# First stage of the next image's conv transform: two row combinations on VectorE, GpSimd's later sums behind a gate

## The chip, the cores and the metric

The kernel runs on one core of a Trainium2 chip. The metric is the device time of one execution in microseconds (us); where several executions are timed, the median counts. In what follows PE is TensorE, PEld its weight loads, DVE is VectorE, ACT is ScalarE, POOL is GpSimd, and SP the engine whose queue issues most of the DMAs.

## The reference, cut to what matters

Four images of 256 channels and 48x48 pixels, in float32, pass through two layers; each adds its result to its input.

```python
# layer 0
x = x + proj(attention(qkv(relu(bn(conv3x3(gn(x)))))))      # 8 heads, 2304 tokens per image
# layer 1
g = gn(x)
w = conv3x3(g, W_cat)                                       # 45 maps: 5 dilations x 9 taps
cat = [g] + [sum_k softmax(w_d)[k] * shift(g, tap k of dilation d) for d in (1, 6, 12, 24, 36)]
x = x + batchnorm(conv1x1(concat(cat), W_scale))            # statistics over all four images
```

`gn` is a group norm over groups of 8 channels. `bn` uses given statistics, the last batch norm those of its own input.

## The kernel before

**Stages.** The images go through a software pipeline. For each image b there is a conv with the qkv products (`conv_qkv`), then attention (`attention`), then the filters of layer 1 (`dynamic_filters`). Two of these overlap: while the filters of image b-1 are computed, the conv and qkv of image b are the stream `other`, from which `run(ns)` and `drive` pull matmuls to fill TensorE. So there are three changes from one attention to the next mixed stage, after the attention of images 0, 1 and 2. I call them transitions. After the attention of image 3 only the filters are left (`alone`).

**The conv of images 1 to 3** (`Blocks`, `conv_blocks`) is done in a transformed domain in both directions. Rows first: `self.d` holds six views of the normalized image (every fourth row, offset 0 to 5, each 2 x 12 x 50 elements per partition), and `stage0`, `scaled` and `rest` combine them into six row results `v[0]` to `v[5]`, with `v[6]` as scratch. Then columns: `along(i)` forms from `v[i]` four arrays (j = 1, 2, 0, 3), which are the moving operands of the matmuls for row result i (L1178). The order of i is `ORDER = (1, 2, 3, 4, 0, 5)`; each i takes two tiles (the two halves of the output channels), each tile four steps j, each step two matmuls into one of two PSUM buffers (tag "c"). A step's result is taken out by ACT for the first j (`one`, L1193) and by DVE for the others (L1203, L1204, L1214, L1216). The stream hands back control twice a step, after each matmul, and reports 486 ns each time; a tile is 8 such pieces.

**Where stage0 runs.** `following[0]` is called in `attention` after the last matmuls on the numerators and ahead of `close(last)`, which normalizes the last part of the attention (two DVE transposes around a reciprocal, L1420 to L1430). It builds `Blocks` and calls `stage0` (L1022). In it ACT multiplies two views by 4 (L1025, L1026), and POOL does everything else through `sum` (L1018, two instructions each, one per half of the channels) and `along` (L1096, four instructions): v[3], v[0], v[5], v[1], then the column sums of v[1], then v[2]. The row results live in the memory of the old q and k, so all this waits until the last scores of the attention are done.

**What follows on TensorE.** The last chunk of the projection (L1465), the statistics of the group norm of layer 1 (`norm.finish`: L675 for the mean, L686 and L687 for the variance, with ACT and DVE work between), the normalization of the image in place (two parts of 24 rows; DVE takes one half of the channels, L648, ACT the other, L2116), and then the weights conv (L1547), which needs the whole normalized image. Between these steps `run` pulls conv matmuls: 1000 ns after the local statistics (three matmuls), 1000 ns after the mean (three), 1900 ns after the first part of the normalization (four), 2900 ns after the second (six). These are 16 matmuls, two tiles, all with i = 1. The column sums of the second row result, `along(ORDER[1])`, are issued in the first of those tiles (in `conv_blocks`, at the first matmul), so they stand on POOL's queue right behind stage0. After that `drive` takes over: it runs several streams, each with its own due times from a hand-kept clock (`Clock`), and the order of instructions on every engine is fixed by it when the kernel is built. `rest` is one of these streams.

Of the kernel before, what the change touches and what calls it, by code (L numbers as in the profile page):

```python
# [8 lines left out]
F32 = mybir.dt.float32  # L9
F32R = mybir.dt.float32r  # L10
AF = mybir.ActivationFunctionType
ALU = mybir.AluOpType
# [3 lines left out]
B, C, HH, WW = 4, 256, 48, 48  # L16
N = HH * WW
P = 128
# [40 lines left out]
def conv_preact_kernel(  # L59
# [12 lines left out]
    nc = tc.nc  # L72

    const = ctx.enter_context(tc.tile_pool(name="const", bufs=1))
    small = ctx.enter_context(tc.tile_pool(name="small", bufs=2))
# [477 lines left out]
    with tc.tile_pool(name="w", bufs=1) as wpool, tc.tile_pool(  # L553
        name="act", bufs=1
# [432 lines left out]
        class Blocks:  # L987
# [34 lines left out]
            def stage0(self):  # L1022

                v, d = self.v, self.d
                nc.scalar.mul(v[0], d[2], 4.0)  # L1025
                nc.scalar.mul(v[5], d[1], 4.0)  # L1026
                self.sum(v[3], d[4], d[2], ALU.subtract)
                self.sum(v[0], d[4], v[0], ALU.subtract)
                self.sum(v[5], d[3], v[5], ALU.subtract)
                self.sum(v[1], v[0], v[5], ALU.add)  # L1030
                self.along(1)
                self.sum(v[2], v[0], v[5], ALU.subtract)

            def scaled(self):

# [74 lines left out]
        def conv_blocks(b, psum_tile, blocks, pool, hid):  # L1110

            axpy = blocks.axpy
            tt = nc.vector.tensor_tensor
            rows = hid.rearrange("p h (t r w) -> p h t r w", r=4, w=WW)
            spare = list(blocks.spare)

            results, last = [], [0.0]

            def busy_dve():
                return clock.t["DVE"] > max(clock.t["ACT"], clock.t["PE"]) + 500  # L1120

            def relu(o, r, y, end):
                results.append((o, r, y, end))

            def relus(limit):
                while results and results[0][3] + 150 <= limit:
                    o, r, y, end = results.pop(0)
                    nc.scalar.activation(  # L1128
                        rows[:, o, :, r, :], rows_of(y), AF.Relu,
                        bias=bn_t[:, o : o + 1], scale=bn_s12[:, o : o + 1],  # L1130
                    )
                    clock("ACT", 660, end)

            def before(i, o):

                s12, d12, s34, d34 = (blocks.held[:, j, o] for j in range(4))
                if i == 0:
                    t = spare.pop(0)
                    axpy(t, s34, -4.0, s12)
                    relu(o, 2, t, clock.both(800))  # L1140
                    either(s12, s12, s34, ALU.subtract)
                elif i == 5:
                    t = spare.pop(0)
                    axpy(t, d34, -2.0, d12)
                    relu(o, 1, t, clock.both(800))
                    axpy(d12, d34, -8.0, d12)
                    clock.both(800)

            def target(i, o):

                if i in (1, 3):
                    return blocks.first[o]
                if i in (2, 4):
                    return blocks.held[:, 1 if i == 2 else 3, o]
                return spare.pop(0)

            def after(i, o, y):

                s12, d12, s34, d34 = (blocks.held[:, j, o] for j in range(4))
                if i in (2, 4):  # L1160
                    s, d = (s12, d12) if i == 2 else (s34, d34)
                    either(s, y, blocks.first[o], ALU.add)
                    either(d, blocks.first[o], y, ALU.subtract)
                elif i in (0, 5):
                    relu(o, i and 3, y, either(y, y, s12 if i == 0 else d12, ALU.add))

            blocks.scaled()
            need[0] = lambda: 150 + max(slot("c", 2), blocks.end[STEPS[0]])
            for t, (i, o) in enumerate(TILES):
                u = us.pop(t)  # L1170
                y = target(i, o).rearrange("p (n s) -> p n s", s=2)
                for n, j in enumerate((1, 2, 0, 3)):
                    m = psum_tile(f"pc_{b}_{i}_{o}_{j}")[:, :XN]
                    clock("PE", 0, slot("c", 2), blocks.end[i, j])
                    z = blocks.of[i].rearrange("p (j h n) -> p j h n", j=4, h=NH)[:, j]
                    relus(max(clock.t["ACT"], clock.t["PE"]))
                    for h in range(NH):
                        nc.tensor.matmul(  # L1178
                            m, u[:, h, j], z[:, h], start=(h == 0), stop=(h == NH - 1)
                        )  # L1180
                        clock("PE", MM * XN / CH)
                        if h == 0:
                            need[0] = lambda: 0.0
                            if n == 0:
                                if t + 2 < len(TILES):
                                    us[t + 2] = taken(t + 2)
                                if t == 0:
                                    blocks.along(ORDER[1])
                                before(i, o)
                            yield MM * XN / CH  # L1190
                    if n == 0:
                        one = pool.tile([P, XN], F32, tag="one", name=f"one_{b}_{i}_{o}")
                        nc.scalar.copy(one, m)  # L1193
                        end = clock("ACT", 400, clock.t["PE"])
                    elif n == 1:
                        two = pool.tile([P, 2, XN], F32, tag="two", name=f"two_{b}_{i}_{o}")
                        if busy_dve():
                            nc.scalar.copy(two[:, 1], m)
                            end = clock("ACT", 400, clock.t["PE"])
                            either(two[:, 0], one, two[:, 1], ALU.add, end)  # L1200
                            either(two[:, 1], one, two[:, 1], ALU.subtract, end)
                        else:
                            tt(two[:, 0], m, one, ALU.add)  # L1203
                            tt(two[:, 1], one, m, ALU.subtract)  # L1204
                            end = clock("DVE", 900, clock.t["PE"], end)
                    else:
                        to = y[:, :, n - 2]
                        if busy_dve():
                            nc.scalar.mul(to, m, 1.0 if j == 0 else -1.0)
                            end = clock("ACT", 450, clock.t["PE"])  # L1210
                            either(to, to, two[:, n - 2], ALU.add, end)
                        else:
                            if j == 0:
                                tt(to, m, two[:, 0], ALU.add)  # L1214
                            else:
                                tt(to, two[:, 1], m, ALU.subtract)  # L1216
                            end = clock("DVE", 480, clock.t["PE"])
                        if n == 3:
                            after(i, o, y.rearrange("p n s -> p (n s)"))
                    free["c"].append(end)  # L1220
                    then = STEPS[4 * t + n + 1] if 4 * t + n + 1 < len(STEPS) else None
                    need[0] = lambda: 150 + max(
                        slot("c", 2), blocks.end.get(then, NEVER) if then else last[0],
                    )
                    if n == 3 and o == NH - 1:
                        blocks.passed.add(i)
                    if then is None:
                        relus(NEVER)
                        last[0] = clock.t["ACT"]
                    yield MM * XN / CH  # L1230
# [253 lines left out]
        def dynamic_filters(b, ao, chunk, norm, other, pools):  # L1484
# [621 lines left out]
                project(b, chunk, ao, pp, norm)  # L2106
                chunk += 1
            table(AF.Sqrt)
            for _ in norm.finish(misc):
                run(1000)  # L2110
            norm.shift_of()
            for part in range(2):
                for h in range(NH):
                    t = inside(gn, h, HH // 2 * part, HH // 2)
                    if h:
                        nc.scalar.activation(  # L2116
                            t, t, AF.Identity, bias=norm.shift[:, h : h + 1],
                            scale=norm.rstd[:, h : h + 1],
                        )
                    else:  # L2120
                        normalize(t, t, norm.mean, norm.rstd, h)
                run((1900, 2900)[part])
                if alone and part == 0:
                    flag_of(misc("pf")[:1, : B * NH])
            clock.level()
# [542 lines left out]
```

## Time and profile before

| | |
|---|---|
| median of 3 runs | 2685.55 us (2680.86 to 2685.71) |
| the profiled execution's own time | 2688.87 us |
| its span, first to last instruction | 2687.1 us |
| PE busy | 2595.5 us (97%) |
| DVE busy | 2077.2 us (77%) |
| ACT busy | 1809.1 us (67%) |
| POOL busy | 809.7 us (30%) |
| mean granted TensorE clock | 0.989 |

The profile is of one execution. A row of the timeline has the start in us from the span's start, the length, the engine, the line of the kernel, the operation, what is written and read with sizes, and how many instructions are merged in it; in brackets stands how long the engine had been idle before it, and what ended that. A matmul in float32 appears as two records. A row of the waits has the waiting engine and line, the releaser, and the total, the count and the longest. A row of windows has the busy time of each engine in that stretch (number of instructions in brackets), then the granted TensorE clock as a share of full speed, the DMA share and GB/s.

### The profile page before, as it was taken

The page shows a single profiled execution, that of the slowest core. Times are in us where ns is not written, and L with a number is a line of the kernel's source. Part 1 is how long each engine was busy: PE and PEld are TensorE (multiplying, and loading weights), DVE is VectorE, ACT ScalarE, POOL GpSimd, SP SyncE. Part 2 cuts the span into 40 slices and gives each one's busy share as a digit, 9 for nine tenths or more (in the row PEclk, how much of TensorE's full clock was granted, in tenths as well). Part 3 has the DMA queues.
Part 4 walks back from the last instruction along what each step waited for, and adds up shares of the span by engine and source line. Part 5 has one row for each costly group of instructions (what it writes and reads, how often), then busy time and mean ns, then how long its engine had stood idle before and what let it go on. Part 6 is the DMA issues. An engine that isn't in the chain of part 4 may idle for free. (4 is left out here: it accounts for less than half of the span.)

```text
span 2687.1 us, 42567 instructions
## 1 busy us (share of the span) xinstructions
PE 2595.5 (97%) x16952; PEld 1097.6 (41%) x16952; DVE 2077.2 (77%) x2033; ACT 1809.1 (67%) x2287; POOL 809.7 (30%) x893
## 2 busy tenths in 40 slices
PE   7999999999999999999999999999989999999996
PEld 5632222555562222355555222245546222235554
DVE  7768898758739998957774988894776889895676
ACT  4479898734449999854445998984444889885344
POOL 4201100476520001067750001007765010100453
PEclk9999999999999999999999999999999999999998
DMA  4815445323253445423324354442324544432456
GB/s 173 227 38 107 102 101 117 89 63 103 69 108 73 101 105 110 101 73 86 94 66 90 90 112 102 102 104 78 82 74 119 135 100 101 102 88 76 122 165 221
DMA packets 138094, 279.96 MB, mean 104 GB/s; under 512 B 58152, under 2 KB 98512, under 8 KB 136864
## 3 DMA queue, kind: packets, MB, share of 16 engines
q0 software_dynamic: 27408, 144.00, 23.3%
q1 hardware_dynamic: 110480, 133.17, 18.4%
q8 instruction: 135, 2.21, 0.3%
q14 instruction: 71, 0.58, 0.1%
HBM read 112.12 MB, written 36.04 MB: 55 GB/s over the span
## 5 line engine op out<-in xcount | busy, mean ns | idle before, releaser
L1392 DVE TENSOR_TENSOR acc<-acc,p 128x2048 f32<-128x2048 f32 (+1 forms) x568 | 1039.3, 1830 | 96.2 <-ACT p L1353 44.2
L1353 ACT ACTIVATE p<-se 128x1536 f32<-128x1536 f32 x648 | 937.6, 1447 | 0.0
L1342 PE MATMUL se<-q,k 32*128 32x512 f32 (+1 forms) x4320 | 737.1, 593 | 0.0
L1342 PE MATMUL so<-q,k 32*128 32x512 f32 (+1 forms) x1440 | 728.3, 593 | 3.2 <-DVE bound L1297 2.0
L1377 PE MATMUL num<-p,vT 128*32 128x512 f32 (+1 forms) x5760 | 699.4, 561 | 1.7 <-ACT ao L1402 1.7
L1352 ACT ACTIVATE p<-so 128x512 f32<-128x512 f32 x648 | 388.9, 600 | 158.8 <-PE se L1342 63.1
L1845 POOL TENSOR_TENSOR near<-near,prod 128x384 f32<-128x384 f32 x352 | 353.2, 1036 | 254.8 <-DVE prod L1839 248.8
L1342 PEld LDWEIGHTS so<-q,k 32*128 32x128 f32 x1440 | 216.5, 183 | 517.8 <-ACT p L1352 477.0
L1396 POOL DMA_DIRECT2D ring<-p x128 | 109.2, 853 | 800.9 <-ACT p L1353 589.4
L1377 PEld LDWEIGHTS num<-p,vT 128*32 128x32 f32 x5760 | 128.9, 108 | 475.1 <-issue 448.5
L1839 DVE TENSOR_TENSOR prod<-wb,pad 128x768 f32<-128x768 f32 x192 | 182.0, 954 | 84.9 <-ACT wb L1826 54.1
L1342 PEld LDWEIGHTS se<-q,k 32*128 32x128 f32 x4320 | 227.2, 183 | 5.1 <-ACT p L1353 4.3
L1826 ACT COPY wb<-ws 128x384 f32<-128x384 f32 x216 | 108.5, 505 | 164.9 <-DVE prod L1839 124.2
L1394 POOL DMA_DIRECT2D ring<-p x36 | 20.2, 560 | 569.5 <-ACT p L1353 284.8
L2003 PE MATMUL py<-far,wsc 128*128 128x384 f32 x512 | 169.9, 487 | 0.0
L1547 PE MATMUL pg<-pad,wcat 128*45 128x384 f32 x864 | 147.8, 493 | 8.5 <-ACT lg L1605 8.5
L1258 PE MATMUL pq<-hid,wqkv 128*128 128x384 f32 x384 | 132.7, 500 | 14.2 <-ACT hid L1128 12.0
L1515 ACT COPY far<-far 128x512 f32<-128x512 f32 x86 | 90.3, 1108 | 81.4 <-PE far L1773 77.9
L2003 PEld LDWEIGHTS py<-far,wsc 128*128 128x128 f32 x512 | 96.2, 190 | 66.0 <-issue 1.8
L1258 PEld LDWEIGHTS pq<-hid,wqkv 128*128 128x128 f32 x384 | 73.1, 194 | 68.4 <-ACT hid L1128 14.3
L1392 DVE TENSOR_TENSOR acc<-p,p 128x2048 f32<-128x2048 f32 x36 | 82.3, 2285 | 21.5 <-ACT p L1353 14.6
L1747 DVE COPY_PREDICATED amat<-along_y,bmat 128x768 f32<-128x768 uint32 x72 | 94.7, 1315 | 2.4
(336 smaller groups left out, 2874.0 us busy)
## 6 DMA issues: line engine op xcount, KB each, us to landing
ring<-p POOLq DMA_DIRECT2D x164, 768.0 KB, 5.7
ws<-w_d SPq DMA_DIRECT2D x216, 192.0 KB
ring<-u_d SPq DMA_DIRECT2D x36, 512.0 KB
pad<-in_x SPq DMA_DIRECT2D x14, 1152.0 KB
xst<-in_x POOLq DMA_DIRECT2D x36, 192.0 KB, 3.5
x_d<-pad SPq DMA_DIRECT2D x36, 192.0 KB
u_d<-pad SPq DMA_DIRECT2D x12, 512.0 KB
y_d<-y SPq DMA_DIRECT2D x13, 384.0 KB
```

The lines of the kernel that those rows point to most:

```text
L1258: nc.tensor.matmul(pq[:, :CH], wqkv[:, i, s, g * P : (g + 1) * P], hid[:, i, cols], start=(i == 0), stop=(i == NH - 1),)
L1342: nc.tensor.matmul(dst[:, at : at + n], k_[r, g, m * P : (m + 1) * P], q[r, g, q0 : q0 + n], start=True, stop=True,)
L1352: nc.scalar.activation(p[:, 0, :], s1, AF.Exp, scale=QS)
L1353: nc.scalar.activation(p[:, 1:, :], s3, AF.Exp, scale=QS)
L1377: nc.tensor.matmul(st["num"][r, at : at + n], vT[:, m, g * P + j * D : g * P + (j + 1) * D], p[:, j, at : at + n], start=(m == 0 and not s ...
L1392: nc.vector.tensor_tensor(st["acc"][:, js], other[:, js], p[:, js], ALU.add)
L1396: nc.gpsimd.dma_start(out=extra, in_=p[:, 1:], accum_op=ALU.add)
L1547: nc.tensor.matmul(pg[64 * s : 64 * s + NG, :CH], wcat[:, ii, k, :], shifted(ii, cc, k // 3 - 1, k % 3 - 1), start=(i == 0 and k == 0), st ...
L1826: nc.scalar.copy(pw[:, :CH], fetched[c, k][0])
L1839: nc.vector.tensor_tensor(prod.rearrange("p h (r w) -> p h r w", w=WW), wb, src, ALU.mult)
L1845: nc.gpsimd.tensor_tensor(cat[:, h], cat[:, h], prod[:, h], ALU.add)
L2003: nc.tensor.matmul(py[c][:, o, :CH], wsc[:, n * NH + i, o * P : (o + 1) * P], rhs, start=(n == 0 and i == 0), stop=(n == order[-1] and i = ...
```

## The change

Four edits. (1) In `stage0`, v[0] = d[4] - 4 d[2] and v[5] = d[3] - 4 d[1] are each computed by two DVE instructions (scalar_tensor_tensor) instead of an ACT multiplication and two POOL subtractions; v[3] goes to the end of the stage. (2) `along(ORDER[1])` is issued in the last step of the second tile instead of the first step of the first. (3) Where another conv is running beside the filters, the first `run` of the norm takes 2500 ns (six matmuls) instead of 1000 (three), and the last takes 1400 ns (three) instead of 2900 (six); the total of 16 stays. (4) After the second part of the normalization is issued, one POOL instruction on a single element per partition reads one element of the first and one of the last row that DVE normalizes, so that POOL waits there until both parts are done.

```diff
             def stage0(self):
 
                 v, d = self.v, self.d
-                nc.scalar.mul(v[0], d[2], 4.0)
-                nc.scalar.mul(v[5], d[1], 4.0)
-                self.sum(v[3], d[4], d[2], ALU.subtract)
-                self.sum(v[0], d[4], v[0], ALU.subtract)
-                self.sum(v[5], d[3], v[5], ALU.subtract)
+                self.axpy(v[0], d[2], -4.0, d[4])
+                self.axpy(v[5], d[1], -4.0, d[3])
                 self.sum(v[1], v[0], v[5], ALU.add)
                 self.along(1)
                 self.sum(v[2], v[0], v[5], ALU.subtract)
+                self.sum(v[3], d[4], d[2], ALU.subtract)
...
                         if h == 0:
                             need[0] = lambda: 0.0
+                            if t == 1 and n == 3:
+                                blocks.along(ORDER[1])
                             if n == 0:
                                 if t + 2 < len(TILES):
                                     us[t + 2] = taken(t + 2)
-                                if t == 0:
-                                    blocks.along(ORDER[1])
                                 before(i, o)
...
             table(AF.Sqrt)
-            for _ in norm.finish(misc):
-                run(1000)
+            for i, _ in enumerate(norm.finish(misc)):
+                run(1000 if i or alone else 2500)
             norm.shift_of()
...
-                run((1900, 2900)[part])
+                if part:
+                    gate = small.tile([P, 1], F32, tag="gate", name=f"gate_{b}")
+                    nc.gpsimd.tensor_tensor(
+                        gate, gn[:, 0, 1, 1:2], gn[:, 0, HH, 1:2], ALU.add
+                    )
+                run((1900, 2900 if alone else 1400)[part])
```

`axpy`, called by stage0 now, existed already: for each half of the channels it issues `nc.vector.scalar_tensor_tensor(out, in0=x, scalar=a, in1=y, op0=mult, op1=add)`.

## The prediction on record

> **What bounds the kernel now.** The page first. Its row of busy times says that TensorE has little to give:
>
> ```profile
> PE 2595.5 (97%) x16952; PEld 1097.6 (41%) x16952; DVE 2077.2 (77%) x2033; ACT 1809.1 (67%) x2287; POOL 809.7 (30%) x893
> ```
>
> PE idles for 92 us in all, so an edit pays only where PE waits. The waits of PE sorted by cause name the place: `PE pc L1178 <- POOL cv_v L1096`, 7.1 us in 3 times, one per transition. The PE timeline of the first transition, from the projection (L1465) to the weights conv (L1547), shows it:
>
> ```profile
> 519.35 2.85 PE L1465 MATMUL pp<-ao,wp 128*128 128x384 f32 x8
> 524.58 1.86 PE L1178 MATMUL pc<-cv_v,ring 128*128 128x288 f32 x6 [2.38 <-POOL cv_v L1096]
> 526.27 0.28 PE L675 MATMUL pm_n<-mvn,gmat 128*128 128x2 f32 x2
> 526.41 1.70 PE L1178 MATMUL pc<-cv_v,ring 128*128 128x288 f32 x6
> 527.95 0.28 PE L686 MATMUL pv_n<-mvn,gmat 128*128 128x2 f32 x2
> ...
> 531.77 3.45 PE L1178 MATMUL pc<-cv_v,ring 128*128 128x288 f32 x12 [1.27 <-DVE cv_k L1216]
> 535.15 2.16 PE L1547 MATMUL pg<-pad,wcat 128*45 128x384 f32 x12
> ```
>
> The bracket on the second row is the gap: the projection ends at 522.20, the first conv matmul starts at 524.58. POOL's timeline says why:
>
> ```profile
> 511.14 4.04 POOL L1018 TENSOR_TENSOR cv_k<-pad 128x600 f32<-128x600 f32 x2 [9.09 <-issue]
> 515.14 5.32 POOL L1018 TENSOR_TENSOR cv_q<-pad,cv_q 128x600 f32<-128x600 f32 x4
> 520.42 2.86 POOL L1018 TENSOR_TENSOR cv_k<-cv_q 128x600 f32<-128x600 f32 x2
> 523.36 4.53 POOL L1096 TENSOR_TENSOR cv_v<-cv_k 128x576 f32<-128x576 f32 x4
> ```
>
> From top to bottom: v[3], then v[0] and v[5], then v[1], then its column sums; without pause, so the first column sum is ready only at 523.36 + 1.17. From DVE's timeline, the slack and the normalization:
>
> ```profile
> 510.08 2.29 DVE L1392 TENSOR_TENSOR acc<-acc,p 128x2048 f32<-128x2048 f32 x1
> 516.13 0.72 DVE L1420 STREAM_TRANSPOSE rt<-den 128x512 f32<-128x512 f32 x1 [3.76 <-PE den L1408]
> ...
> 529.14 2.21 DVE L648 TENSOR_SCALAR pad<-pad,gmean_n,grstd_n 128x1152 f32<-128x1152 f32 x1
> ```
>
> DVE is free from 512.37 to 516.13. Its L648 takes 2.21 here, and by its list of durations 0.86 to 2.21 for one shape: POOL is running beside it. Last, the busy times by stretch for the second transition; the column to see is the third from the right, the granted clock:
>
> ```profile
> 1171.50:1173.70 2.20, 0.00 (x0) 0.00 (x0) 2.13 (x4) 0.00 (x0) 2.12 (x3) 1.00 0.28 61
> 1173.70:1179.00 5.30, 5.22 (x17) 3.83 (x17) 1.29 (x5) 1.07 (x5) 5.30 (x6) 0.68 0.50 148
> ```
>
> In half-microsecond stretches the clock is 0.50 from about 1175.0 to 1178.3. The third transition has the same after its gap (0.69), the first has not (1.00).
>
> **What the Trainium skill says.** "TensorE: Matmul & The Clock Gate", Part 1: TensorE falls to half clock after an idle window of about 3.4 us, the window is free-running, and full clock returns after a busy one. The trace agrees on the length (3.3 us at 0.50) and on the element of chance (two of three like gaps), but gaps of 2.36 us were enough. "SBUF — State Buffer", Who interferes with whom: a DVE instruction with two SBUF inputs, or a tensor_scalar in a two-port mode, and a GpSimd instruction that reads SBUF exclude each other for the whole instruction. The trace agrees: L1076, the DVE form that the change adds, takes 0.75 us (128x576) and up to 1.55, and L648 spreads as said.
>
> **The change, part by part.** I count from the end of the projection to the start of L1547. Before: T1 522.20 to 535.15 = 12.95; T2 1171.42 to 1185.59 = 14.17; T3 1824.22 to 1837.73 = 13.51; sum 40.63 us.
>
> *v[0] and v[5] on DVE.* Four instructions of 128x600. Nearest rows: L1076 0.75 for 576 elements, L877 0.78 for 600 with two SBUF inputs. I take 0.775, so 3.1 us, in the 3.76 us ahead of the transpose; queued behind them is `close(last)`, for which PE waits. POOL has nothing to do until the third one ends (512.37 + 2.33 = 514.70), so only the fourth can collide with it; if that takes 1.55 the transpose starts 0.1 to 0.2 late. I take 0.15 per transition. Ends: 0 (as now) and, if all four take 1.55, 6.2 - 3.76 = 2.4. ACT loses two multiplications of 1.21, worth nothing: it idles 6.7 us right after.
>
> *POOL's start.* v[1] at 514.8, two of 1.46 plus at most 0.8 of collision: done by 518.5; the first column sum 1.17 later, 519.7. PE needs it at 522.20, so 2.5 us of cover, and the next sums come every 1.17 while PE uses one per 1.13. The gap goes.
>
> *Matmuls reordered.* From 524.58 to 526.27 three conv matmuls take 1.69: 0.563 each. Now, from the projection's end: six, 3.38; mean matmuls 0.14 (526.27 to 526.41); some 0.1 for the buffer that DVE frees with L1204; three, 1.69; the variance matmuls start at 5.31 and take 0.36; three more reach 7.36. The seventh after the variance needs the buffer that ACT's L1193 frees, and that stands behind ACT's first half of the normalization. Before, L686 started at 527.95 and this L1193 ended at 531.29, 3.34 later; so now at 8.65 to 8.71. PE waits 1.35, then four matmuls, 2.25: L1547 could start at 10.96. The wait for L1216 (1.27 in T1) is thus not saved but replaced. The local statistics that the mean matmuls need end at 524.95 = 2.75, hidden by the six matmuls.
>
> *Gate and held sums.* L648's second part follows L1204 at about 9.55; with POOL held it takes 0.86 to 1.36: 10.4 to 10.9, just inside. Without the gate it could take 2.2, and L1547 would be 0.8 late; that is what the gate is worth. Queued behind the gate on POOL: `along(ORDER[1])` (4.6 us) and `rest` (first six sums 8.9). Gate at about 533.1 in T1, so they end at 546.6 instead of 545.05. The first to need the sums is the third tile at 545.53, now some 2 us sooner: they are ready at 537.7, 6 us of cover. After `rest`'s third result POOL is next released at 551.87 (by DVE), now about 550: 3.4 us of cover. The gate itself is one element. DMAs: the weights of the second tile land by 517.5 (525 needed); the DMAs that tiles issue on SP keep their places. The build clock gets the same POOL additions ahead of `drive`, so I expect the same order after it.
>
> *Sum.* 10.96 + 0.15, rounded to 11.1, three times: 33.3 against 40.63: 7.3 us, of which T1 1.85, T2 3.07, T3 2.41. Of it half clock: the six matmuls around the mean took 4.76 in T2 and 4.63 in T3 against 3.23 in T1, so 1.53 + 1.40 = 2.93. The profiled execution, 2688.87 (1.8 around its span), would become 2681.6. It lies 3.3 above the median of the runs, which may well hold fewer half-clock windows. I count the 4.4 that don't depend on the clock and about 2.1 of the 2.9: 2685.55 - 6.5 = **2679.0**.
>
> **Does it last?** In the conv stage behind each transition the waits of PE are small (largest there: L1258 for ACT 2.2 to 6.1, L1547 2.3), and all follow PE's own work; so a shift lasts until attention, where ACT and PE go in step.
>
> **The rivals.** About 0.2% (5.4 us) is what a measurement can tell from no change here.
>
> *Larger:* the 1.35 wait for L1193 doesn't arise, because ACT or the buffers come earlier than I read. 3 x 1.35 = 4.05 more: **2675.0**. For it: T3 before waits only 0.36. Against: ACT's order is fixed, 0.48 + 1.35 us stand ahead.
>
> *Given back as half clock elsewhere:* 0.50 also shows near 645, 735, 1230, 1385, 1865 and 1950, a window costing about 3.3 x 0.5 = 1.7. Shifts move the work against the windows; one more per mixed stage gives back 5.1: **2684.1**. Against: it may as well go the other way.
>
> *Slower: the DVE work is not covered.* If the four instructions take 1.55, `close` and the projection move 2.4 us, the gap only moves ahead of the projection, and all three transitions pay half clock: 3 x (10.96 + 2.44) = 40.2, with 3 x 1.5 for the clock (as above) 44.7 against 40.63: **2689.6**. It decides from 0.94 us each, where 3.76 is used up, and loses from about 1.4. For it: L1076 beside POOL. Against: POOL has nothing to read before the third ends.
>
> *The change doesn't do what it says:* if POOL began late because the DVE results wait for the numerators' end (516.9), the first sum would be there at about 524, saving nearly nothing; but POOL began at 511.14 on the same memory, so I give this no chance of its own.
>
> **How the numbers follow.** Likeliest (2676 to 2682) 0.58; larger 0.15; given back 0.21; slower 0.06. Faster by over 0.2% (under 2680.2): 0.45 of the likeliest, all of the larger, 0.02 of the given back: 0.62. Slower by over 0.2% (above 2690.9): 0.04. The rest 0.34. The range runs from 2674.5 to 2685.0; outside lie half of the larger, the slower case and 0.06 of the given back.
>
> **What would show it.** PE's row behind L1465 without a bracket, and its start within 0.1 of the projection's end; four DVE rows between L1392 and L1420, with L1420's idle time near 0.6 and its start at most 0.2 late against L1392; clock 1.00 at all three transitions; L1547 11.1 after the projection's end; a wait of about 1.35 for ACT L1193; L648 at 0.86 to 1.36; POOL's `along` behind L648. Wrong would be: L1420 over a microsecond late, PE waiting for POOL at the third tile (L1096 into hid), or transitions shorter as said with the sum gone.

## The result and the profile after

| | before | after |
|---|---|---|
| median | 2685.06 us (14 runs, 2680.02 to 2688.80) | 2677.47 us (14 runs, 2673.73 to 2681.37) |
| profiled execution, span | 2688.87, 2687.1 | 2675.02, 2673.2 |
| granted TensorE clock, mean | 0.989 | 0.992 |
| projection's end to L1547 (after: L1545), T1 / T2 / T3 | 12.95 / 14.17 / 13.51 | 10.61 / 10.61 / 10.61 |

The medians lie 7.6 us apart. The ratio after to before is 0.9974, interval 0.9966 to 0.9981, which is 7.0 us (5.1 to 9.1): faster by a little over the 0.2% that can be told. Ratios leave out runs more than 1.5% above a kernel's fastest; in e1 and e2 below these are taken for the runs that show the effect most, so there I go by the median and the spread of all runs. Behind `stage0` the lines of the kernel after stand two lower: L1465 is L1463, L1178 is L1176, L1547 is L1545.

PE's timeline of the first transition after the change; in the brackets, how long PE had been idle and what ended that:

```profile
519.17 2.85 PE L1463 MATMUL pp<-ao,wp 128*128 128x384 f32 x8
521.86 3.07 PE L1176 MATMUL pc<-cv_v,ring 128*128 128x288 f32 x12
524.84 0.38 PE L675 MATMUL pm_n<-mvn,gmat 128*128 128x2 f32 x2
525.60 1.69 PE L1176 MATMUL pc<-cv_v,ring 128*128 128x288 f32 x6 [0.38 <-DVE two L1202]
527.12 0.28 PE L686 MATMUL pv_n<-mvn,gmat 128*128 128x2 f32 x2
...
527.49 1.70 PE L1176 MATMUL pc<-cv_v,ring 128*128 128x288 f32 x6
530.49 2.21 PE L1176 MATMUL pc<-cv_v,ring 128*128 128x288 f32 x8 [1.30 <-ACT one L1191]
532.63 2.16 PE L1545 MATMUL pg<-pad,wcat 128*45 128x384 f32 x12
```

The conv matmul behind the projection has no bracket any more: the 2.38 us for POOL are gone. In the place of the 1.27 us for L1216 stand 1.30 us for ACT, and 0.38 us for DVE's L1202 are new. POOL and DVE at the same time:

```profile
514.43 3.29 POOL L1018 TENSOR_TENSOR cv_k<-cv_q 128x600 f32<-128x600 f32 x2 [12.58 <-DVE cv_q L1074]
517.80 4.52 POOL L1094 TENSOR_TENSOR cv_v<-cv_k 128x576 f32<-128x576 f32 x4
522.28 2.92 POOL L1018 TENSOR_TENSOR cv_k<-cv_q 128x600 f32<-128x600 f32 x2
525.15 2.89 POOL L1018 TENSOR_TENSOR cv_k<-pad 128x600 f32<-128x600 f32 x2
532.16 0.19 POOL L2122 TENSOR_TENSOR gate<-pad 128x1 f32<-128x1 f32 x1 [4.12 <-DVE pad L648]
532.31 4.80 POOL L1094 TENSOR_TENSOR hid<-cv_k 128x576 f32<-128x576 f32 x4
```

```profile
512.11 2.86 DVE L1074 SCALAR_TENSOR_TENSOR cv_q<-pad 128x600 f32<-128x600 f32 x4
515.95 0.72 DVE L1418 STREAM_TRANSPOSE rt<-den 128x512 f32<-128x512 f32 x1 [0.98 <-PE den L1406]
...
528.30 0.88 DVE L648 TENSOR_SCALAR pad<-pad,gmean_n,grstd_n 128x1152 f32<-128x1152 f32 x1
530.47 0.46 DVE L1201 TENSOR_TENSOR two<-pc,one 128x288 f32<-128x288 f32 x1 [1.29 <-ACT one L1191]
```

POOL starts v[1] 2.3 us behind the start of the first DVE row (before: 520.42, now 514.43), v[1]'s sums start at 517.80 instead of 523.36, and POOL is still from 528.04 to 532.16, held by the gate while DVE normalizes in 0.88. The row of busy times by stretch for the second transition has the clock third from the right, now 1.00:

```profile
1169.00:1174.00 5.00, 4.62 (x23) 3.41 (x21) 3.82 (x10) 1.07 (x5) 5.00 (x4) 1.00 0.66 179
```

**Where the time went.** The three transitions lost 8.80 us (40.63 to 31.83). The two profiled executions differ by 13.9; in stretches of 5 us, the one before had about three more with a clock below 0.99 elsewhere, at about 1.7 each, which makes up the rest. The medians differ by 7.6. Outside the transitions, and `stage0` just ahead of them, every engine has the same instructions in the same order in the two profiles, but for one gate more after the attention of image 3.

### The profile page after: what moved, and what is told of

The parts are those of the page before. It is cut to its first block, busy times and chain, and to the rows that moved or that the text cites. A ratio compares the mean times of both kernels' runs of the same rounds, so it can differ in the third digit from the quotient of the medians.

```text
span 2673.2 us, 42578 instructions
## 1 busy us (share of the span) xinstructions
PE 2586.6 (97%) x16952; PEld 1092.1 (41%) x16952; DVE 2080.8 (78%) x2045; ACT 1802.6 (67%) x2281; POOL 789.6 (30%) x885
## 3 DMA queue, kind: packets, MB, share of 16 engines
q8 instruction: 135, 2.21, 0.3%
## 5 line engine op out<-in xcount | busy, mean ns | idle before, releaser
L1545 PE MATMUL pg<-pad,wcat 128*45 128x384 f32 x864 | 146.7, 490 | 8.8 <-ACT lg L1603 8.8
```

The source lines that it names most:

```text
L1545: nc.tensor.matmul(pg[64 * s : 64 * s + NG, :CH], wcat[:, ii, k, :], shifted(ii, cc, k // 3 - 1, k % 3 - 1), start=(i == 0 and k == 0), st ...
```

## The experiments

Two theories. **A**, the one on record: the gain is the early start of v[1] plus the new order of the matmuls, and the gate is worth 0.8 us at most. **B**: the gate does more than that, or the rows on DVE cost more than I saw. All runs are timed beside the kernel before on the same chip; its median there lay between 2683.4 and 2685.9. There were four chips: one for e1 to e4, one for e7 to e10, one for e6, e11 and e12, one for e13. Comparisons between these groups are comparisons across chips.

### e1: the rows alone

```diff
-                nc.scalar.mul(v[0], d[2], 4.0)
-                nc.scalar.mul(v[5], d[1], 4.0)
-                self.sum(v[3], d[4], d[2], ALU.subtract)
-                self.sum(v[0], d[4], v[0], ALU.subtract)
-                self.sum(v[5], d[3], v[5], ALU.subtract)
+                self.axpy(v[0], d[2], -4.0, d[4])
+                self.axpy(v[5], d[1], -4.0, d[3])
...
+                self.sum(v[3], d[4], d[2], ALU.subtract)
```

Against the kernel before; edits 2 to 4 are left out.

> Only the first edit: v[0] and v[5] by DVE, v[3] last; the matmuls are taken 3, 3, 4, 6 as before, no gate. Theory (each edit has its own wait): the gap of 2.4 us behind the projection goes and the half clock with it, but three matmuls end 1.7 us after the projection and the local statistics only at 2.75, so PE waits about 1.0 for DVE L672 ahead of the mean matmuls; and L648 runs beside POOL (up to 2.2 us), so the wait for L1214 of about 1.3 stays. From the projection's end to the weights conv 11.9 us per transition, against 10.61 with all edits: about 4 us slower than the changed kernel, 3 to 6 faster than the one before. Rival (the DVE rows alone are the gain): 10.6 per transition, as fast as the changed kernel.

Measured: median 2695.65 us (22 runs, 2675.56 to 2722.78), slower than before. But the runs lie in groups: ten from 2675.6 to 2684.1, six from 2695.3 to 2698.9, five from 2707.3 to 2712.7, one at 2722.8. The profiled execution was of the first group (2681.58): transitions of 11.54 to 11.57 and this wait ahead of the mean matmuls, which edit 3 covers:

```profile
525.00 0.38 PE L675 MATMUL pm_n<-mvn,gmat 128*128 128x2 f32 x2 [1.36 <-DVE mvn L672]
```

So of the 8.8 us, edit 1 saves 6.0 (40.63 to 34.66), when nothing happens. In 12 runs of 22 something costs 12 to 16 us, once or more; no profile holds it here, e2 shows what it is likely to be.

### e2: rows and order, no gate

```diff
...
-                if part:
-                    gate = small.tile([P, 1], F32, tag="gate", name=f"gate_{b}")
-                    nc.gpsimd.tensor_tensor(
-                        gate, gn[:, 0, 1, 1:2], gn[:, 0, HH, 1:2], ALU.add
-                    )
```

Against the kernel after, of which edits 1 and 3 are left: edit 2 is undone too (the lines left out above are those shown at e9). By the code, POOL's order without the gate is the same whether edit 2 is made or not; this was not run.

> Edits one and three: DVE rows and the matmuls taken 6, 3, 4, 3, no gate, so that POOL forms the second column sums while DVE normalizes. Theory: the waits ahead of the mean go; L648 takes 1.4 to 2.2 instead of 0.88, its second part ends about 0.5 to 1.3 later, and since the weights conv stands right behind it, a transition takes 11.1 to 11.7 instead of 10.61: 1.5 to 3 us slower than the changed kernel. Rival (the gate does nothing, POOL would not hit DVE there): 10.6, no difference.

Measured: median 2703.05 us (16 runs, 2676.15 to 2722.59). The profiled execution (2687.24) caught it once, in the first transition. PE, DVE and POOL there:

```profile
529.09 1.24 PE L1176 MATMUL pc<-cv_v,ring 128*128 128x288 f32 x4 [1.30 <-ACT one L1191]
540.95 2.29 PE L1176 MATMUL pc<-cv_v,ring 128*128 128x288 f32 x4 [10.62 <-DVE two L1202]
543.17 3.29 PE L1545 MATMUL pg<-pad,wcat 128*45 128x384 f32 x12
```

```profile
526.89 13.28 DVE L648 TENSOR_SCALAR pad<-pad,gmean_n,grstd_n 128x1152 f32<-128x1152 f32 x1
```

```profile
526.57 4.56 POOL L1094 TENSOR_TENSOR hid<-cv_k 128x576 f32<-128x576 f32 x4
531.04 2.89 POOL L1018 TENSOR_TENSOR cv_v<-cv_v,cv_q 128x600 f32<-128x600 f32 x2
533.85 2.89 POOL L1018 TENSOR_TENSOR cv_q<-cv_k,cv_v 128x600 f32<-128x600 f32 x2
536.66 2.89 POOL L1018 TENSOR_TENSOR cv_k<-cv_k,cv_v 128x600 f32<-128x600 f32 x2
```

One instruction of 0.88 us took 13.28. It could not run until POOL had gone through ten instructions one behind another and its queue was empty, at 539.55. PE's bracket of 10.62 names DVE's L1202, which was queued behind it. The transition is 22.6 instead of 10.6, and the clock from 541 to 546, behind so long a gap, is 0.55. In the other two transitions of the same execution L648 took 1.48 and all was well (10.61), with the same instructions ahead of it; so it isn't for a result of POOL's that it waits. This is a **lock-out**, and A is wrong on what the gate is worth. The experiments from e9 to e13 ask what makes it and what ends it.

### e9: the sums of v[2] ahead of the gate

```diff
-                            if t == 1 and n == 3:
-                                blocks.along(ORDER[1])
...
+                                if t == 0:
+                                    blocks.along(ORDER[1])
```

Against the kernel after; edit 2 is undone.

> The changed kernel without the later call of the column sums of v[2]: they stand ahead of the gate on GpSimd instead of behind it. If VectorE is locked out until GpSimd's queue pauses, the lock-out now ends at the gate: L648 at most about 5 us (the four sums take 4.5) instead of 13, and TensorE waits at most 2 to 3 us for it. The median is then 2677 to 2685, with a spread of no more than 10 us and no step of 13. Rival: the gate has no part in ending the lock-out, or the place of the sums has no part in it: either steps of 13 us again (2690 or more), or the changed kernel's own time, 2677, with L648 at 0.9.

Measured: 2691.02 us (10 runs, 2684.16 to 2692.70), ratio 1.0024 (1.0014 to 1.0034). The lock-out is bounded, as expected, but it seems to come nearly always (the profiled execution, 2684.16, is the fastest of the ten and holds two) and it costs more than I wrote: those two transitions take 13.1, and behind the one below the clock is down to 0.72 (1182 to 1186). DVE, POOL and PE in the second transition:

```profile
1173.77 4.86 DVE L648 TENSOR_SCALAR pad<-pad,gmean_n,grstd_n 128x1152 f32<-128x1152 f32 x1
```

```profile
1173.46 4.55 POOL L1094 TENSOR_TENSOR hid<-cv_k 128x576 f32<-128x576 f32 x4
1180.22 0.19 POOL L2122 TENSOR_TENSOR gate<-pad 128x1 f32<-128x1 f32 x1 [2.22 <-DVE pad L648]
```

```profile
1179.40 1.24 PE L1176 MATMUL pc<-cv_v,ring 128*128 128x288 f32 x4 [2.21 <-DVE two L1202]
```

L648 ends 0.6 us after the fourth sum, just where POOL stops at the gate. So POOL's pause ends it; and edit 2, which by the code changes nothing alone, keeps the four sums of v[2] from L648. It doesn't keep stage0 from it: in e6 below, where v[3] ends later, the first part of L648 took 1.9 in spite of the gate.

### e8: v[3] ahead of v[2], no gate

```diff
-                self.sum(v[2], v[0], v[5], ALU.subtract)
                 self.sum(v[3], d[4], d[2], ALU.subtract)
+                self.sum(v[2], v[0], v[5], ALU.subtract)
```

Against e2.

> The second experiment (VectorE's rows and the new order, no gate) with two GpSimd steps exchanged: v[3] ahead of v[2]. Then the column sums of v[2] follow directly on the instruction whose result they read and must wait for its end, as in the kernel before. Theory: VectorE's L648 is locked out for 13 us only when GpSimd has a run of instructions none of which waits for the one directly ahead of it; here it gets in at the latest between v[2] and its sums, within 2.9 us. Then no steps of 13 us: L648 at most 3 us, all runs within about 8 us of each other, median 2677 to 2682. Rival: the lock-out is a matter of chance whenever GpSimd is busy, or of the new moment at which L648 starts, and v[3]'s place has no part in it: L648 of 10 us or more in some transitions, runs again spread over 2676 to 2722 with steps of 13 us, median 2690 to 2705.

Measured: 2678.06 us (22 runs, 2674.91 to 2681.93), ratio 0.9979 (0.9973 to 0.9986). No steps; L648 at most 1.60. On the chip of e9, exchanging two POOL steps does what the gate does. POOL's rows of the first transition:

```profile
525.31 2.87 POOL L1018 TENSOR_TENSOR cv_k<-cv_q 128x600 f32<-128x600 f32 x2
528.26 5.57 POOL L1094 TENSOR_TENSOR hid<-cv_k 128x576 f32<-128x576 f32 x4
```

v[2] ends at 528.18 and its sums start at 528.26: they wait 0.08 for the result directly ahead. In e2 the sums follow on v[3] without such a gap (v[3]'s row ends at 526.64, theirs starts at 526.57). One thing doesn't fit my wording, though: L648 came at 528.45, after that wait, in the middle of four sums that wait for nothing, and got in at the next boundary all the same. So it may be the wait, or the moment at which L648 comes: 0.2 us after the start of the first sum here, 0.3 in e2. e11 keeps the moment of e2, e12 takes a third one.

### e11: one pause, no gate

```diff
                         self.end[i, j] = clock("POOL", 1400)
+                        if i == ORDER[1] and j == js[0]:
+                            stop = small.tile([P, 1], F32, tag="stop", name=f"stop_{self.b}")
+                            nc.gpsimd.tensor_tensor(
+                                stop, to[:, 0, 0, 0:1], to[:, 0, 0, 1:2], ALU.add
+                            )
```

Against e2.

> The second experiment (rows and order, no gate, GpSimd's order as in the change, so with lock-outs) with one GpSimd instruction of a single element added behind the first of the four column sums of v[2]; it reads that sum, so GpSimd must wait for the end of the instruction directly ahead, once. L648 arrives 0.3 us after the start of that sum. Theory: the lock-out lasts as long as GpSimd's instructions follow without such a wait, and any one wait ends it. Then L648 gets in at the wait, about 0.8 us after it arrives, and takes at most about 1.8 us; no run above 2685, median 2677 to 2680, though nothing holds GpSimd back for VectorE. Rival: the wait is too short to matter, and only an empty or a held queue ends the lock-out: L648 of 10 to 13 us in some transitions, runs spread from 2676 to 2722, median 2690 to 2705.

Measured: 2678.48 us (14 runs, 2675.92 to 2680.61), ratio 0.9982 (0.9974 to 0.9990); L648 at most 1.53. The whole pause, on POOL:

```profile
528.04 1.16 POOL L1094 TENSOR_TENSOR hid<-cv_k 128x576 f32<-128x576 f32 x1
529.28 0.59 POOL L1098 TENSOR_TENSOR stop<-hid 128x1 f32<-128x1 f32 x1
529.83 3.91 POOL L1094 TENSOR_TENSOR hid<-cv_k 128x576 f32<-128x576 f32 x3
```

From 529.20 to 529.28: 0.08 us without a POOL instruction, and DVE, waiting since 528.32, got in. Nothing was held back until DVE was done. L648 came 0.3 us after the start of the first sum in all three transitions, as in e2. On this chip no kernel ran in which lock-outs were to be expected, so e11 alone doesn't exclude that it has none; but e8, free, and e9, not free, ran on one chip.

### e12: another moment

> The matmuls handed out as in e7 and GpSimd's order as in e8, without the gate. L648 then starts about 0.4 us later than in e8, some 0.5 us after the first column sum of v[2] instead of 0.2. If what kept e8 free of lock-outs is the wait ahead of these sums as such, this one is free as well: median 2674 to 2676, ratio 0.9963, no run above 2682. If it is only the moment at which L648 arrives within GpSimd's instruction (0.2 us after its start in e8, 0.3 us in the experiments with lock-outs), they come back here: runs in steps of 12 to 14 us, median 2680 to 2700. L648 at 1.2 to 1.6 us where it gets in.

The edit is e7's (below) and e8's together, without the gate. Measured: 2674.88 us (6 runs, 2670.61 to 2678.18), ratio 0.9969 (0.9957 to 0.9981), L648 at most 1.14. It came 0.65 to 0.67 us after the start of the first sum, against 0.2 in e8 and 0.3 in e2 and e9. So being free isn't bound to the moment of e8. Together with e11, which is free at the moment of e2, this speaks for the wait and against the moment; e12 alone wouldn't, since it avoids 0.3 as well.

### e10: the kernel before, v[3] last

```diff
-                self.sum(v[3], d[4], d[2], ALU.subtract)
...
                 self.sum(v[2], v[0], v[5], ALU.subtract)
+                self.sum(v[3], d[4], d[2], ALU.subtract)
```

> The kernel before with one line moved: GpSimd computes v[3] behind v[2] instead of first. Nothing goes to VectorE, no order of TensorE changes, no gate. Theory (lock-out behind a run of GpSimd instructions that don't wait for the one directly ahead): L648 of some 10 to 13 us in some transitions, runs in steps of 13 us from 2685 up to 2725, median 2690 to 2710, though less work has moved than in any other experiment. Rival (the lock-out came with VectorE's new rows or with the earlier start of GpSimd's work): no L648 over 3 us, median 2684 to 2687, ratio within 0.1% of 1.

Measured: 2681.20 us (14 runs, 2679.41 to 2700.09). Twelve runs lie from 2679.4 to 2683.5, two at 2698.0 and 2700.1; 39 runs of the unedited kernel beside it reach no more than 2690.8. A median 3 us lower, since v[1] is ready sooner (in T1 PE's gap behind the projection is 1.31 instead of 2.38), and two runs some 18 us slower. That is far rarer than the expected text has it (median 2690 to 2710), and the profile holds no lock-out, so that these two were lock-outs is inferred from the size of the step. If they were, lock-outs are possible without the wait ahead of the run, but v[3]'s place alone doesn't make them frequent: 12 runs of 22 in e1 and 15 runs of 16 in e2 had a step. What does is not shown.

### e13: L648 in another form

```diff
-                        normalize(t, t, norm.mean, norm.rstd, h)
+                        nc.vector.scalar_tensor_tensor(
+                            out=t, in0=t, scalar=norm.mean[:, h : h + 1],
+                            in1=norm.rstd[:, h : h + 1].unsqueeze(2).to_broadcast(
+                                [P, HH // 2, WW]
+                            ),
+                            op0=ALU.subtract, op1=ALU.mult,
+                        )
```

Against e2.

> The second experiment (rows and order, no gate, no pause, the order in which lock-outs came) with L648 issued in another form: a scalar_tensor_tensor that subtracts the mean and multiplies by the reciprocal deviation as a broadcast operand, instead of a tensor_scalar. GpSimd's queue is unchanged. Theory: only some forms of VectorE's instruction have to wait for GpSimd (in the traces L648, a tensor_scalar, and the copy L1515 are stretched beside GpSimd, the tensor_tensors L1201 and L1202 are not, 0.44 to 0.46 us in all of them). Then the new form takes the same time whatever GpSimd does, an estimated 1.2 to 1.5 us from the 0.78 us of 600 elements at L1074, and nothing is ever locked out: median 2677 to 2680, no run over 2685. Rival: any instruction of VectorE of this size can be locked out: durations of 10 us or more, runs spread to 2722, median 2690 to 2705.

My theory fell. Median 2706.12 us (6 runs, 2700.05 to 2723.43), and the profiled execution (2719.74) has a lock-out in each transition:

```profile
528.26 13.88 DVE L2119 SCALAR_TENSOR_TENSOR pad<-pad,gmean_n,grstd_n 128x1152 f32<-128x1152 f32 x1
...
1188.45 13.89 DVE L2119 SCALAR_TENSOR_TENSOR pad<-pad,gmean_n,grstd_n 128x1152 f32<-128x1152 f32 x1
...
1851.56 13.87 DVE L2119 SCALAR_TENSOR_TENSOR pad<-pad,gmean_n,grstd_n 128x1152 f32<-128x1152 f32 x1
```

The mistake was to count L1201 and L1202 as witnesses: they read one operand from PSUM. The new form reads two from SBUF, and of that the Trainium skill ("SBUF — State Buffer", Who interferes with whom) says that it contends with a GpSimd instruction that reads SBUF, just as the two-port tensor_scalar does. The run agrees. With POOL idle the new form takes 1.41 and L648 0.88, so a form that was slower by itself was shut out just as long.

### e3: the change without the rows, and e4: the gap filled

e3 keeps edits 2 to 4 and leaves `stage0` as it was. e4 is the kernel before with four matmuls on constants in the gap:

```diff
             table(AF.Sqrt)
+            if not alone:
+                busy(misc(f"fill_{b}"), 4)
```

> The changed kernel with stage0 as before (ACT and POOL form v[0] and v[5]); order, later column sums and gate stay. Theory: PE waits 2.4 us again behind the projection, with half clock in some transitions; a transition takes 2.4 + 10.6 = 13.0 us, as before (12.95) or a little more with the clock: within 2 us of the kernel before. Rival (order and gate carry the gain): 3 us or more faster than before.

> The kernel before with four idle matmuls (results unused, about 1.9 us) behind the projection in the three transitions, so that PE has no gap of 2.4 us there but starts the conv no sooner. Theory (the gap causes the half clock): clock 1.00 in all transitions, about 12.9 to 13.0 us per transition, and of the 7.6 us of the change only the half clock's share comes: 2 to 3 us faster than before. Rival (half clock comes by chance anywhere, the gap is not its cause): half clock still in some transitions, time as before.

Measured: e3 2689.26 us (22 runs), ratio 1.0016 (1.0010 to 1.0022), with transitions of 12.83, 14.35 and 14.22, and half clock in the last two (0.69 and 0.66 over the stretch): order and gate are worth nothing until v[1] comes sooner. By the ratio e3 is 4.3 us slower than before, where within 2 was expected; its profiled transitions are only 0.8 longer in sum, and where the rest lies was not followed. e4 2681.32 us (22 runs), ratio 0.9988 (0.9982 to 0.9995), though the conv matmuls still start late (12.92, 12.92, 13.29). The rows by stretch, from the first of them on, have the clock at 1.00 in T2 and T3, where before it was 0.68 and 0.69:

```profile
1174.70:1180.00 5.30, 5.30 (x25) 4.09 (x25) 2.64 (x8) 2.17 (x9) 5.30 (x5) 1.00 0.48 138
1825.60:1831.00 5.40, 5.40 (x26) 4.13 (x26) 2.74 (x8) 2.24 (x9) 5.40 (x5) 1.00 0.49 141
```

So keeping PE busy over the gap, with work of no use, is worth 0.0012 of 2685, 3.2 us (1.3 to 4.8; the medians lie 4.6 apart). I had counted 2.1 for it.

### e6: the rows twice

```diff
-                self.axpy(v[0], d[2], -4.0, d[4])
-                self.axpy(v[5], d[1], -4.0, d[3])
+                for _ in range(2):
+                    self.axpy(v[0], d[2], -4.0, d[4])
+                    self.axpy(v[5], d[1], -4.0, d[3])
```

> The changed kernel with VectorE's four instructions at L1074 issued twice, the result unchanged: 3.1 us more on VectorE ahead of the close of the last attention chunk at each transition. In the changed kernel VectorE was idle for 0.98 us ahead of its transposition. If that is all the cover that is left, each close comes 2.1 us later: 6.3 us in all and up to 1.5 us of half clock at each transition, median 2683 to 2688, ratio to before 0.9995 to 1.001. Rival, the rows lie beside other work and the close isn't what TensorE waits for: within 1 us of the changed kernel, ratio 0.997.

Measured: 2680.23 us (13 runs, 2677.65 to 2685.14), ratio 0.9986 (0.9978 to 0.9995), under what I expected. The transposition has no idle time ahead of it now, and PE waits once per transition, ahead of the projection. The second one:

```profile
1171.22 2.82 PE L1464 MATMUL pp<-ao,wp 128*128 128x384 f32 x8 [1.30 <-DVE ao L1429]
```

Eight instructions take 5.63 us, four 2.86: 2.77 more, of which 1.30 reach PE, three times 3.9 us. So in the kernel after the rows had 1.47 us of cover left: the 0.98 on DVE, and some 0.5 more that PE had to spare between the filler matmuls and the projection.

### e7: the matmuls handed out otherwise

```diff
-                run(1000 if i or alone else 2500)
+                run(1000 if alone else (2500, 1500)[i])
...
-                run((1900, 2900 if alone else 1400)[part])
+                run((1900, 2900)[part] if alone else (900, 1900)[part])
```

> The changed kernel with its twelve matmuls handed out differently: a fourth accumulator before the variance, so that TensorE reaches the inputs that wait for ScalarE's L1191 later. In the changed kernel each transition has one wait of 1.30 us for it. If that wait is on the path, it falls to 0.6 to 0.8 us at each of the three transitions, the transitions go from 10.6 to about 10.0 us, and the median is about 2 us below the changed kernel's: 2675.5, ratio to before 0.9965. Rival: the wait is given back, because the accumulators taken later now make the last matmuls wait for VectorE or the weights conv wait for the normalization behind them: transitions stay at 10.6 or grow to 11, ratio 0.997 to 0.998.

Measured: 2674.33 us (6 runs, 2670.18 to 2675.82), ratio 0.9963 (0.9950 to 0.9976), and all three transitions at 9.59, better than the 10.0 expected. PE's rows:

```profile
527.98 2.19 PE L1176 MATMUL pc<-cv_v,ring 128*128 128x288 f32 x8
530.45 1.24 PE L1176 MATMUL pc<-cv_v,ring 128*128 128x288 f32 x4 [0.28 <-DVE two L1202]
531.62 2.49 PE L1545 MATMUL pg<-pad,wcat 128*45 128x384 f32 x12
```

ACT's rows show why:

```profile
527.82 0.40 ACT L1191 COPY one<-pc 128x288 f32<-128x288 f32 x1 [1.89 <-PE pc L1176]
...
529.30 2.60 ACT L2114 ACTIVATE pad<-pad,gshift_n,grstd_n 128x1152 f32<-128x1152 f32 x2
```

A step takes two matmuls. The fourth one behind the mean ends the second tile's first step before the variance, so ACT takes out its result (L1191) ahead of its normalization (L2114). In the kernel after that matmul comes behind the variance, and L1191 stands at 530.06, behind the first part of L2114. So the wait for ACT is not met later, as the expected text has it, but gone; the 0.28 that is left is for DVE's L1202. Both e7 and e12 lie below the kernel after; their intervals overlap its own, so that they beat it rests on the transitions in the traces (9.59 and 9.83 against 10.61), not on the medians alone.

## Why the prediction was right, and where it was not

The change was faster by about the amount forecast, for the reason given. By its own steps:

- *v[0] and v[5] on DVE, 3.1 us in 3.76.* Four took 2.86: 776 to 780 ns each, as taken, but their records overlap, which the sum left out. None collided with POOL: the term of 0.15 is 0. The 0.98 left is what the forecast's "idle time near 0.6" should have been.
- *The slower rival* (DVE work not covered, from 0.94 us each): with the 1.47 us of cover that e6 shows, it decides from about 1.08 us each instead. The mechanism is real, since e6 shows it, and is not reached.
- *POOL's start.* v[1] at 514.43 (forecast 514.8), first sum ready at about 519.0 (519.7). The gap went.
- *Matmuls reordered.* The mean matmuls start 2.82 behind the projection's end, forecast 3.38. The rate of 0.563 per matmul came from a run of three behind an idle PE; six, right behind the projection, took 0.50 each (521.86 to 524.84). Of this little is gained: PE then waits 0.38 for L1202 (forecast 0.1) and 1.30 for ACT (forecast 1.35), and L1545 comes at 10.61 instead of 11.1. The matmul that waits for ACT is called the seventh after the variance; it is the fourth after it and the seventh after the mean. The sum has it in the right place.
- *Half clock.* Taken at 2.1 us of 2.9; e4 puts it at 3.2 by itself. With the transitions 0.49 shorter each, the forecast would have been 6.5 + 1.5 + 1.1 = 9.1; the medians show 7.6 and the ratio 7.0, with an interval of 5.1 to 9.1. So with its terms set right the sum is at the edge of what was measured. That 6.5 lies nearer is in part luck: the terms that were too small stand against a shortfall whose place is not known.
- *The larger rival* said that the wait for ACT would not arise. It arose; e7 shows that it can be taken out, for 1.0 us per transition. *Given back as half clock elsewhere* did not happen in the profiled execution, which went the other way; over all runs it isn't known, and it could be that shortfall.

**The step that failed** is *Gate and held sums*: "Without the gate it could take 2.2, and L1547 would be 0.8 late; that is what the gate is worth." I bounded L648 by the longest that the trace of before had, 2.21, of which 1.6 is waiting: little more than one POOL instruction. When nothing locks DVE out, the gate is worth less than that: the two transitions of e2 without a lock-out take 10.61 with no gate, those of e8 10.67. But edit 1 moves v[3] between v[2] and v[2]'s sums, and with it goes the one wait on POOL that stood ahead of the run of ten. Without a gate L648 then takes up to 13.28, and the median is 18 us (e1) or 26 us (e2) above the kernel after. e8 puts the wait back and is free; e10 says that its loss alone brings few lock-outs. So the rows on DVE, alone, would have been a loss, and the prediction of a kernel with edits 1 to 3 would have been wrong by some ten times the 2.4 that its three terms come to. It didn't show because the gate was there, for a reason that the prediction didn't know: here its being right is luck. To take the longest that the trace of before held for the longest that can be was the fault: in that trace L648 got in at the first or second boundary every time.

## What to carry to other kernels

Here a VectorE instruction that GpSimd can block was held not by one GpSimd instruction (1.2 to 1.5 us) but by a run of ten (12.7 us), up to the first pause; so look at what stands ahead of such a run before moving work into it, and put a dependence or a gate there. Runs that lie in groups some 15 us apart say that something happens by chance: sort the runs before reading a profile, which may be of a lucky one. When a wait is only replaced by another (1.27 by 1.30 here), look at which buffer it is for, and at what its reader has to do first: a different hand-out of the same matmuls was worth another 3 us by the transitions.

## What the runs showed of the hardware

**The lock-out.** The Trainium skill ("SBUF — State Buffer", Who interferes with whom) says that whoever issues first has the pair for its whole instruction and the other blocks fully. Here DVE stayed blocked for ten instructions of POOL (L648 took 13.28 us in e2), though at the first of their boundaries it had already waited 0.87 us. In the transitions without a lock-out, boundaries that came 0.15 to 0.23 us after L648 were too early, and it got in at the first that came 0.35 us or more after it; a column sum of POOL behind it took 1.66 instead of 1.17.

**What goes with it.** In the single records, POOL's next instruction starts a little before the last one's end. From the instruction on that was running when L648 came, start of the next minus end of the last, in ns:

```
e2  T1   L648 13.28   -79 -78 -82 -83 -84 -83 -84 -85 -85, queue empty
e2  T2   L648  1.48   -36, in
e9  T1   L648  1.48   -55, in
e9  T2   L648  4.86   -67 -67 -70, gate
e9  T3   L648  4.88   -87 -87 -95, gate
e11 T3   L648  1.53   (ahead of it -69 -78 -81 -83)  +79, in
e8  T1   L648  1.59   (ahead of it -33 -33, the wait +79)  -43, in
e13 T1  L2119 13.88   -65 -64 -58 -58 -59 -58 -59 -60 -61, queue empty
e13 T3  L2119 13.87   -41 -42 -40 -35 -35 -35 -35 -34 -35, queue empty
```

In a run without a wait the overlap drifts, in some transitions from 40 to over 80 ns; a wait on the instruction directly ahead (+79) sets it back to about 40. Leaving out the boundaries that were too early, L648 got in at 39 with 31 to 55 ns and at one with 67, over all profiles, and at every pause; it did not get in at 15 with 67 to 95, which belong to three lock-outs. The other form (e13) was shut out at 58 to 78 in two transitions, but in the third at 34 to 42, where L648 always got in. So for L648 the lock-out goes with the overlap, and a pause ends both; but a large overlap is not needed for every lock-out, so it can't be the whole cause. What the cause is, and what makes the overlap drift, stays open.
